# A gated recurrence's bias products on 128 rows, its first block's inputs step by step, and the modulation's products first among the filler

## Chip, cores and metric

One core of a Trainium2 chip. The metric is the device time of one execution in microseconds; lower is better. The kernel before took 1380.88 us, the median of three runs.

## The reference

The whole computation is a quantised feed-forward layer behind a gated recurrence, and behind that a transformer block in hyperbolic geometry with adaptive modulation. What the change touches is the recurrence over 64 steps for a batch of 128, and the modulation vector:

```python
def _L0_cond_ref(h_t, z, W, b, alpha):
    Wh, Wz = W[:, :D], W[:, D:]
    leak = 1.0 - alpha
    def step(h, z_t):
        gate = jax.nn.sigmoid(h @ Wh.T + z_t @ Wz.T + b)
        h_new = jnp.tanh(h * leak + gate * z_t)
        return (h_new, h_new)
    _, hs = jax.lax.scan(step, h_t, jnp.swapaxes(z, 0, 1))
    return jnp.swapaxes(hs, 0, 1)

def _L0_ffn_ref(x, clip_x, ...):
    scale = sigmoid(clip_x) * jnp.max(jnp.abs(x)) / 127.0
...
ada = t_emb @ w_ada + b_ada
sh_msa, sc_msa, g_msa, sh_mlp, sc_mlp, g_mlp = jnp.split(ada, 6, axis=-1)
```

D is 256. t_emb is the conditioning vector, which is also the recurrence's first state. The maximum in the feed-forward layer runs over the whole output of the recurrence, so nothing of that layer can be quantised before step 63 is done.

## The kernel before

**Stages.** The kernel runs the recurrence first (the scan, some 200 us), then the first feed-forward layer up to its global maximum, then a long fused pipeline. Only the scan's code is touched. All DMAs are issued from one queue, SP's, in order.

**The scan.** The state is kept transposed: 256 features lie on 128 partitions in two halves (index c), the batch of 128 along the free dimension. Steps are handled in blocks of four (TS = 4, index n for the block, i for the step in it, t = 4n + i). For each block there are two PSUM tiles pg, one for each half, 128 x 512: four steps of 128 columns.

- z_parts(n) (L406 to L417) puts the input's share into both tiles of a block: for each half one bias product (L413: gate3, the bias split into three bf16 parts on 3 rows, times a tile of ones) and two f32 products of 512 columns (L415). It is a generator that yields after each f32 product. For block 0 it runs to its end before the loop (L419) and leaves the bias product out; later blocks are advanced by one yield in each step of the block before (L451), the rest at the block's end (L461).
- A step adds the state's share: four f32 products of 128 columns (L434; a profile shows each f32 product as two records, so x8). In block 0 two bias products of 128 columns follow (L438).
- Then for each half: sigmoid on ACT (L442), times the input on DVE (L444), plus leak times the old state on DVE (L445), tanh on ACT (L446). L434 of the next step needs the result. L447 keeps a running maximum for the step.

gate3's three rows come by three small DMAs (L206) once DVE has split the bias.

**Filler work.** Everything else that has to be prepared is issued between the steps by a planner in the loop (L452 to L460). There are two generators, products() and pieces(); each yields its pieces with a cost for DVE, ACT and PE. Each step adds a fixed room for each generator (products: 0.3, 0.3, 0.55), and pieces are taken until the room of one engine is used up. products() starts at step 3. The engines run in program order, so a piece lies just behind the step that issued it.

products() holds three things, in this order before the change: the product of two feed-forward weights with each other and with a second weight (L346, wide f32 products of 256 columns, with weights from w_f1T and w_f2), the same weights with a bias (L360, an output of one row; L362 copies it on ACT); the split of that row into three on GpSimd (L364 with L192 and L194, then three DMAs at L365) with a small sum of squares (bsq, L368 to L371); and the modulation (L375 to L391): for each half w of ada, a load of w_ada and of the bias b_ada into the tile ba, six f32 products (L383), three DVE additions into ba (L386, L388), and one DMA that writes ba eight times over to DRAM, 3 MB (L390).

w_f1T, w_f2 and the two halves of w_ada share two buffers (stage2, L233). ba has one buffer, so the second half's load waits until the first half's write has read it.

pieces() quantises and transposes the other weights (L240 to L245 and L92).

**After the scan.** L469 to L473 form the global maximum and its inverse, isx. L488 quantises the states. Its tiles take over the memory of the scan's set-up tiles, which are given back there.

Of the kernel before, what the change touches and what calls it, by code (L numbers as in the profile page):

```python
# [11 lines left out]
F32 = mybir.dt.float32  # L12
F32R = mybir.dt.float32r
BF16 = mybir.dt.bfloat16
# [3 lines left out]
ALU = mybir.AluOpType  # L18
# [4 lines left out]
P = 128  # L23
B, T, D = 128, 64, 256
# [19 lines left out]
AR = 8  # L44
TS = 4
# [25 lines left out]
def tile_kernel(ctx, tc, a, out):  # L71
    nc = tc.nc
    V, S, G_, PE = nc.vector, nc.scalar, nc.gpsimd, nc.tensor
# [68 lines left out]
    with ExitStack() as l0:  # L142
# [15 lines left out]
        with ExitStack() as sc_:  # L158
# [36 lines left out]
                    out.append(part)  # L195
                return out

            gate3 = setup.tile([3, D], BF16, name="gate3")
            ones4 = setup.tile([3, TS * B], BF16, name="ones4")
            V.memset(ones4, 1.0)  # L200

            def to_rows3(parts, dst):
# [22 lines left out]
            def bank():  # L225
                return ps_t.tile([P, 512], F32, name="pt", tag="pt")
# [6 lines left out]
            def stage2(shape, src):  # L233
                t = setup.tile(shape, F32, name="st2", tag="stage2", bufs=2)
                dma(out=t, in_=src)
                return t
# [95 lines left out]
            def products():  # L332

                b1T = setup.tile([P, 8], F32, name="b1T")
                dma(out=b1T, in_=a["b_f1T"])
                s1 = stage2([P, 8, D], a["w_f1T"].rearrange("(c p) k -> p c k", p=P))
                s2 = stage2([P, 8, D], a["w_f2"].rearrange("(c p) k -> p c k", p=P))  # L340
                r2 = setup.tile([1, 2 * D], F32, name="r2")
                for w, s_ in ((0, s1), (1, s2)):
                    pt = bank()
                    for c in range(2):
                        for k in range(8):
                            PE.matmul(pt[:, c * D : (c + 1) * D], lhsT=s1[:, k, c * P : (c + 1) * P],  # L346
                                      rhs=s_[:, k, :], start=(k == 0), stop=(k == 7))
                            yield 0, 0, 0.43
                    gst = setup.tile([P, 2, D], F32, name="gst", tag="gst", bufs=2)
                    S.copy(gst.rearrange("p c k -> p (c k)"), pt)  # L350
                    if w == 0:
                        S.activation(gst[:, 0, P:], pt[:, P:D], AF.Copy, scale=2.0)
                    yield 0, 0.52 + 0.3 * (1 - w), 0
                    for c in range(2):
                        sl = slice(w * D, (w + 1) * D)
                        split((wm[:, 0, c, sl], wm[:, 1, c, sl]), gst[:, c, :])
                        yield 0, 0.35, 0
                    pt = bank()
                    for k in range(8):
                        PE.matmul(pt[:1, :D], lhsT=b1T[:, k : k + 1], rhs=s_[:, k, :], start=(k == 0), stop=(k == 7))  # L360
                        yield 0, 0, 0.43
                    S.activation(r2[:, w * D : (w + 1) * D], pt[:1, :D], AF.Copy, scale=2.0 - w)  # L362
                    yield 0, 0.3, 0
                for i, part in enumerate(split3(r2, 1, G_)):  # L364
                    dma(out=rows3[64 + i : 65 + i, :], in_=part)  # L365
                bsq = setup.tile([P, 8], F32, name="bsq")
                bs1 = setup.tile([P, 1], F32, name="bs1")
                S.activation(bsq, b1T, AF.Square, accum_out=bs1)  # L368
                pt = bank()
                PE.matmul(pt[:, :1], lhsT=ones, rhs=bs1, start=True, stop=True)  # L370
                V.tensor_copy(bb2, pt[:, :1])  # L371
                yield 0.15, 0.3, 0.1


                for w in range(2):  # L375
                    st = stage2([P, 2, 3 * D], a["w_ada"].rearrange("(c p) k -> p c k", p=P)[:, :, w * 3 * D : (w + 1) * 3 * D])
                    ba = setup.tile([P, 3 * D], F32, name="ba", tag="ba", bufs=1)
                    dma(out=ba, in_=a["b_ada"][w * 3 * D : (w + 1) * 3 * D].partition_broadcast(P))
                    for q in range(3):
                        sl = slice(q * D, (q + 1) * D)  # L380
                        pt = bank()
                        for k in range(2):
                            PE.matmul(pt[:, :D], lhsT=h0T[:, k, :], rhs=st[:, k, sl], start=(k == 0), stop=(k == 1))  # L383
                            yield 0, 0, 0.43
                        if q == 1:
                            V.scalar_tensor_tensor(ba[:, sl], pt[:, :D], 1.0, ba[:, sl], ALU.add, ALU.add)  # L386
                        else:
                            V.tensor_tensor(ba[:, sl], pt[:, :D], ba[:, sl], ALU.add)  # L388
                        yield 0.35, 0, 0
                    dma(out=ada_d[:, :, w * 3 * D : (w + 1) * 3 * D],  # L390
                        in_=ba.unsqueeze(1).broadcast_to((P, AR, 3 * D)))  # L391


            vas = []
            for i in range(4):
                va = ep.tile([P, H, 2, HV], F32, name=f"va{i}", tag=f"va{i}", bufs=1)
# [6 lines left out]
            todo, left = [products(), pieces()], [[0.0] * 3] * 2  # L403
            pgs = {}

            def z_parts(n):  # L406

                pgs[n] = [ps_z.tile([P, TS * B], F32, name=f"pg{c}", tag=f"pg{c}") for c in range(2)]
                for c in range(2):
                    sl = slice(c * P, (c + 1) * P)  # L410

                    if n:
                        PE.matmul(pgs[n][c], lhsT=gate3[:, sl], rhs=ones4, start=True, stop=False)  # L413
                    for k in range(2):
                        PE.matmul(pgs[n][c], lhsT=WT[:, 2 + k, sl], rhs=xts[n][:, k, :],  # L415
                                  start=(n == 0 and k == 0), stop=(k == 1))
                        yield  # L417

            for _ in z_parts(0):  # L419
                pass  # L420
            for n in range(T // TS):
                if n + 2 < T // TS:
                    load_x(n + 2)
                xt = xts[n]
                pg = pgs.pop(n)
                ahead = z_parts(n + 1) if n + 1 < T // TS else iter(())
                for i in range(TS):
                    t = n * TS + i
                    st = slice(i * B, (i + 1) * B)
                    z = xt[:, :, st]  # L430
                    hp = h0T if t == 0 else hsT[:, :, t - 1, :]
                    for k in range(2):
                        for c in range(2):
                            lp = PE.matmul(pg[c][:, st], lhsT=WT[:, k, c * P : (c + 1) * P], rhs=hp[:, k, :],  # L434
                                           start=False, stop=False, skip_group_check=True)
                    if n == 0:
                        for c in range(2):
                            lp = PE.matmul(pg[c][:, st], lhsT=gate3[:, c * P : (c + 1) * P], rhs=ones4[:, :B],  # L438
                                           start=False, stop=False, skip_group_check=True)
                    for c in range(2):  # L440
                        gate = wk.tile([P, B], F32, name="gate", tag=f"gate{c}", bufs=2)
                        S.activation(gate, pg[c][:, st], AF.Sigmoid)  # L442
                        with tc.issue_after(lv.ins) if c else nullcontext():
                            V.tensor_tensor(gate, gate, z[:, c, :], ALU.mult)  # L444
                        lv = V.scalar_tensor_tensor(gate, hp[:, c, :], leak[:, c : c + 1], gate, ALU.mult, ALU.add)  # L445
                        ls = S.activation(hsT[:, c, t, :], gate, AF.Tanh)  # L446
                    V.tensor_reduce(hmax[:, t : t + 1], hsT[:, :, t, :], AX.XY, ALU.max,  # L447
                                    apply_absolute_value=True)

                    with tc.issue_after(lv.ins), tc.issue_after(ls.ins), tc.issue_after(lp.ins):  # L450
                        next(ahead, None)  # L451
                        for q in range(2):  # L452
                            if t < CFG["hold"][q]:
                                continue
                            left[q] = [min(l, 0.0) + r for l, r in zip(left[q], CFG["room"][q])]
                            while min(left[q]) > 0:
                                cost = next(todo[q], None)
                                if cost is None:
                                    break
                                left[q] = [l - c for l, c in zip(left[q], cost)]  # L460
                for _ in ahead:  # L461
                    pass
# [765 lines left out]
```

## Time and profile before

| what | us |
|---|---|
| median of three runs | 1380.88 |
| lowest and highest | 1379.86, 1386.22 |
| profiled execution, its own time | 1374.36 |
| its span, first to last instruction | 1372.6 |
| first sigmoid (step 0) | 14.28 |
| first sigmoid of step 4 | 25.87 |
| first sigmoid of step 61 | 186.29 |
| last running maximum of the scan (L447) ends | 195.22 |
| first L488 | 201.66 |

Times inside an execution are counted from the span's start. A line of the chain of waits gives start, length and the work on the chain; a line of the timeline gives start, length, engine, line, operation, tiles, shapes and count. Records of one line that follow each other are merged there, with the count behind the x. PE stands for matmuls on TensorE, PEld for its weight loads, SPq for the DMA queue's issues, ACT for the scalar engine, DVE for the vector engine and POOL for GpSimd.

### The profile page before, as it was taken

What the parts mean: (1) busy time and instruction counts of PE and PEld (TensorE: products, weight loads), DVE (VectorE), ACT (ScalarE), POOL (GpSimd) and SP (SyncE); (2) the same over time, 40 slices, a digit from 0 to 9 for tenths busy, and PEclk for the clock granted to TensorE, in tenths of its full rate; (3) what the DMA queues carried; (4) which work ended last, traced back from release to release, by engine and by line L of the source; (5) the groups of instructions that cost most, each with busy time, mean ns of one, the idle gap of its engine ahead of it and who ended that gap; (6) DMA issues with size and microseconds to landing.
All of it is one profiled execution on the core that took longest, in us unless ns stands there. A gap on an engine that the chain in (4) does not pass through costs nothing.

```text
span 1372.6 us, 23851 instructions
## 1 busy us (share of the span) xinstructions
PE 1096.8 (80%) x7380; PEld 744.0 (54%) x7380; DVE 1145.4 (83%) x3544; ACT 827.0 (60%) x2428; POOL 844.6 (62%) x1043
## 2 busy tenths in 40 slices
PE   7999957984589789878879798888887888964654
PEld 4656542332366566655657576666655656643442
DVE  5666669997778787888998999999899989899573
ACT  2545438982377568666768666776675777752331
POOL 3111207865688766687868878686686785765441
PEclk9999989995599789889999798997998989986765
DMA  7112245669733441233344334322414231323211
GB/s 236 54 54 85 70 196 195 257 265 283 225 96 120 124 145 49 90 116 117 98 130 125 116 113 146 108 92 90 126 63 124 70 104 51 97 74 96 72 47 46
DMA packets 119306, 163.66 MB, mean 119 GB/s; under 512 B 10885, under 2 KB 72074, under 8 KB 119178
## 3 DMA queue, kind: packets, MB, share of 16 engines
q1 hardware_dynamic: 119178, 162.13, 37.0%
q8 instruction: 58, 0.95, 0.3%
q14 instruction: 70, 0.57, 0.1%
HBM read 115.94 MB, written 46.14 MB: 118 GB/s over the span
## 4 chain that ended last, share of the span: by engine, by line
DVE 44%; PE 21%; POOL 14%; DMA 8%; issue 6%; ACT 6%; SPq 1%; POOLq 0%; DVEq 0%; ACTq 0%
DMA ada<-ada_d 5%; PE pg L434 4%; DVE u L797 4%; PE pg L415 3%; DVE u L724 2%; DVE u L725 2%; DVE junk L743 2%; DVE nh L920 2%; DVE u L618 2%; DVE bn L703 2%; DVE u L1052 2%; POOL r L640 2%; PE pgate L527 1%; PE qk L915 1%; POOL u L737 1%
## 5 line engine op out<-in xcount | busy, mean ns | idle before, releaser
L609 ACT ACTIVATE junk<-u 128x256 bf16<-128x256 f32 x432 | 183.8, 428 | 162.1 <-DVE u L725 49.4
L915 PE MATMUL qk<-wqkv,uT 128*128 128x512 f32 (+1 forms) x768 | 194.8, 391 | 12.3 <-DVE uT L906 6.4
L737 POOL TENSOR_TENSOR u<-u,ada 128x256 f32<-128x256 f32 x128 | 105.7, 827 | 80.9 <-ACT junk L609 73.4
L915 PEld LDWEIGHTS qk<-wqkv,uT 128*128 128x128 f32 x768 | 132.9, 209 | 40.2 <-DVE uT L906 12.1
L966 PE MATMUL sc<-qM,kT 64*64 64x256 f32 x1024 | 128.1, 419 | 20.9 <-ACT kT L956 11.6
L1040 PE MATMUL ml<-wm,uT 128*128 128x512 f32 (+1 forms) x384 | 120.9, 454 | 0.0
L983 PE MATMUL ao<-va,e 128*64 128x34 f32 x2048 | 90.1, 241 | 32.9 <-DVE u L1014 17.8
L983 PEld LDWEIGHTS ao<-va,e 128*64 128x64 f32 x2048 | 79.5, 155 | 59.6 <-DVE u L1014 19.4
L1040 PEld LDWEIGHTS ml<-wm,uT 128*128 128x128 f32 x384 | 83.7, 221 | 47.3 <-issue 25.3
L616 ACT ACTIVATE qM<-sc,mhead 128x256 f32<-128x256 f32 x256 | 102.0, 495 | 11.5 <-PE sc L92 11.3
L880 PE MATMUL dn<-wdT,hq 128*128 128x256 bf16 (+1 forms) x384 | 66.3, 314 | 45.9 <-DVE x L882 20.4
L513 POOL TENSOR_TENSOR hv<-uv,sil 128x512 f32<-128x512 f32 x44 | 57.6, 1312 | 66.2 <-DVE am L516 48.5
L945 POOL TENSOR_TENSOR va<-qkv,comb 64x256 f32<-64x256 f32 x128 | 88.3, 690 | 9.9 <-PE ao L983 4.2
L966 PEld LDWEIGHTS sc<-qM,kT 64*64 64x64 f32 x1024 | 56.5, 143 | 63.1 <-ACT kT L956 17.7
L609 ACT ACTIVATION_READ_ACCUMULATOR junk<-u 128x1 f32 x432 | 87.9, 203 | 0.0
L974 ACT ACTIVATE e<-sc 128x512 f32<-128x512 f32 x128 | 74.7, 606 | 19.4 <-PE ao L983 9.7
L434 PE MATMUL pg<-hsT,WT 128*128 128x128 f32 x504 | 75.3, 289 | 9.4 <-ACT hsT L446 9.0
L434 PEld LDWEIGHTS pg<-hsT,WT 128*128 128x128 f32 x504 | 64.7, 191 | 31.4 <-ACT hsT L446 28.6
L1094 PE MATMUL fp<-wfT,yT 128*128 128x256 f32 x256 | 78.7, 439 | 0.0
L941 POOL TENSOR_TENSOR qkv<-qkv,comb 128x512 f32<-128x512 f32 x64 | 70.2, 1110 | 12.3 <-DVE comb L932 3.0
L620 POOL TENSOR_SCALAR hb<-hl,cu 128x1280 int8<-128x1280 f32 x64 | 64.2, 1008 | 21.4 <-DMA hl<-h_d 14.0
L880 PEld LDWEIGHTS <-hq 128*128 128x128 bf16 (+1 forms) x384 | 37.2, 108 | 73.1 <-issue 37.5
(286 smaller groups left out, 3192.6 us busy)
## 6 DMA issues: line engine op xcount, KB each, us to landing
ada<-ada_d SPq DMA_DIRECT2D x128, 256.0 KB, 3.5
h_d<-hv SPq DMA_DIRECT2D x80, 256.0 KB, 2.1
hl<-h_d SPq DMA_DIRECT2D x32, 640.0 KB, 4.3
ada<-ada_d SPq DMA_DIRECT2D x128, 128.0 KB, 2.4
xt<-in_xT_dram SPq DMA_DIRECT2D x16, 512.0 KB, 4.5
xr<-in_x_dram SPq DMA_DIRECT2D x32, 256.0 KB, 4.3
x_d<-x SPq DMA_DIRECT2D x32, 256.0 KB, 3.1
xt<-x_d SPq DMA_DIRECT2D x32, 256.0 KB, 2.8
```

The source lines that it names most:

```text
L434: lp = PE.matmul(pg[c][:, st], lhsT=WT[:, k, c * P : (c + 1) * P], rhs=hp[:, k, :], start=False, stop=False, skip_group_check=True)
L609: S.activation(junk, src, AF.Square, accum_out=acc)
L616: S.activation(dst, src, AF.Copy, scale=by)
L737: ENG[pick(f"gate{which}", g)].tensor_tensor(av, av, gb, ALU.mult)
L880: PE.matmul(py[:, i * D : (i + 1) * D], lhsT=hq[r, j, i * P : (i + 1) * P], rhs=wdT[r, j, :], start=(i == 0 and j == 0), stop=(j == 5), sk ...
L915: PE.matmul(pm[:, :n_], lhsT=uT[:, z, k, cs], rhs=wqkv[:, w, k, lo:hi], start=False, stop=(k == 1 and q == 2))
L945: ENG[pick("va", g)].tensor_tensor(va[r, :, s, 0:HD], qkv[r, xy, 512:768].rearrange("p (h d) -> p h d", d=HD), bc_in(comb[r, xy * 48 + 32 ...
L966: PE.matmul(sc[rr][s * T : (s + 1) * T, c * 256 : (c + 1) * 256].rearrange("p (v t) -> p v t", v=4), lhsT=kTs[xy][r, c, s * T : (s + 1) * ...
L974: S.activation(e.rearrange("p c v t -> p (c v t)"), sc[rr], AF.Exp, scale=1.0 / math.sqrt(HD))
L983: PE.matmul(pv[xy * T : (xy + 1) * T, hh], lhsT=E[2 * xy + hh // 4][:, c, hh % 4, :], rhs=vas[(2 * h2 + xy) % 4][:, c * 8 + hh], start=Tru ...
L1040: PE.matmul(pm[:, cs], lhsT=uT[:, z, k, i * P : (i + 1) * P], rhs=wm[:, w, k, cs], start=False, stop=(k == 1 and q == 2))
L1094: PE.matmul(o, lhsT=yT[:, 2 * i + c, :], rhs=wfT[:, c, :], start=False, stop=(c == 1))
```

## The change

It has three parts.

1. gate3 and ones4 become tiles of 128 rows. gate3 is filled with zeros first, and its three rows are written as before; the bias products multiply 128 rows, of which 125 add zero.
2. Block 0's inputs are multiplied step by step. z_first(i) issues four f32 products of 128 columns: step 0's before the loop, the next step's within each step. z_parts is used from block 1 on alone, and in block 0 it is advanced from step 1 on, not from step 0 on.
3. The modulation's loop moves to the front of products(), unchanged but for ba, which gets two buffers.

```diff
-            gate3 = setup.tile([3, D], BF16, name="gate3")
-            ones4 = setup.tile([3, TS * B], BF16, name="ones4")
+            gate3 = setup.tile([P, D], BF16, name="gate3")
+            V.memset(gate3, 0.0)
+            ones4 = setup.tile([P, TS * B], BF16, name="ones4")
...
             def products():
+                for w in range(2):
+                    st = stage2([P, 2, 3 * D], a["w_ada"]...)
+                    ba = setup.tile([P, 3 * D], F32, name="ba", tag="ba", bufs=2)
...
+                    dma(out=ada_d[:, :, w * 3 * D : (w + 1) * 3 * D],
+                        in_=ba.unsqueeze(1).broadcast_to((P, AR, 3 * D)))
...
-                for w in range(2):
-                    st = stage2([P, 2, 3 * D], a["w_ada"]...)
-                    ba = setup.tile([P, 3 * D], F32, name="ba", tag="ba", bufs=1)
...
+            def z_first(i):
+                st = slice(i * B, (i + 1) * B)
+                for c in range(2):
+                    for k in range(2):
+                        PE.matmul(pgs[0][c][:, st], lhsT=WT[:, 2 + k, c * P : (c + 1) * P], rhs=xts[0][:, k, st],
+                                  start=(i == 0 and k == 0), stop=False, skip_group_check=True)
+
             def z_parts(n):
...
-                    if n:
-                        PE.matmul(pgs[n][c], lhsT=gate3[:, sl], rhs=ones4, start=True, stop=False)
+                    PE.matmul(pgs[n][c], lhsT=gate3[:, sl], rhs=ones4, start=True, stop=False)
                     for k in range(2):
                         PE.matmul(pgs[n][c], lhsT=WT[:, 2 + k, sl], rhs=xts[n][:, k, :],
-                                  start=(n == 0 and k == 0), stop=(k == 1))
+                                  start=False, stop=(k == 1))
                         yield
 
-            for _ in z_parts(0):
-                pass
+            pgs[0] = [ps_z.tile([P, TS * B], F32, name=f"pg{c}", tag=f"pg{c}") for c in range(2)]
+            z_first(0)
             for n in range(T // TS):
...
-                pg = pgs.pop(n)
+                pg = pgs[n]
...
-                        next(ahead, None)
+                        if n == 0 and i + 1 < TS:
+                            z_first(i + 1)
+                        if n or i:
+                            next(ahead, None)
```

More of the change, by code (lines that the diff above doesn't have):

```diff
@@ L332, in products @@
             def products():
+                for w in range(2):
+                    st = stage2([P, 2, 3 * D], a["w_ada"].rearrange("(c p) k -> p c k", p=P)[:, :, w * 3 * D : (w + 1) * 3 * D])
+                    ba = setup.tile([P, 3 * D], F32, name="ba", tag="ba", bufs=2)
+                    dma(out=ba, in_=a["b_ada"][w * 3 * D : (w + 1) * 3 * D].partition_broadcast(P))
+                    for q in range(3):
+                        sl = slice(q * D, (q + 1) * D)
+                        pt = bank()
+                        for k in range(2):
+                            PE.matmul(pt[:, :D], lhsT=h0T[:, k, :], rhs=st[:, k, sl], start=(k == 0), stop=(k == 1))
+                            yield 0, 0, 0.43
+                        if q == 1:
+                            V.scalar_tensor_tensor(ba[:, sl], pt[:, :D], 1.0, ba[:, sl], ALU.add, ALU.add)
+                        else:
+                            V.tensor_tensor(ba[:, sl], pt[:, :D], ba[:, sl], ALU.add)
+                        yield 0.35, 0, 0
+                    dma(out=ada_d[:, :, w * 3 * D : (w + 1) * 3 * D],
+                        in_=ba.unsqueeze(1).broadcast_to((P, AR, 3 * D)))
                 b1T = setup.tile([P, 8], F32, name="b1T")
@@ L372, in products @@
                 yield 0.15, 0.3, 0.1
-                for w in range(2):
-                    st = stage2([P, 2, 3 * D], a["w_ada"].rearrange("(c p) k -> p c k", p=P)[:, :, w * 3 * D : (w + 1) * 3 * D])
-                    ba = setup.tile([P, 3 * D], F32, name="ba", tag="ba", bufs=1)
[L378 to L391, printed above, removed]
             vas = []
@@ L404, in tile_kernel @@
             pgs = {}
+            def z_first(i):
+                st = slice(i * B, (i + 1) * B)
+                for c in range(2):
+                    for k in range(2):
+                        PE.matmul(pgs[0][c][:, st], lhsT=WT[:, 2 + k, c * P : (c + 1) * P], rhs=xts[0][:, k, st],
+                                  start=(i == 0 and k == 0), stop=False, skip_group_check=True)
             def z_parts(n):
```

## The prediction

> **What bounds the kernel now.** I read the page for the span, then the windows over the recurrent scan, then the chain of waits there, then the timeline at both its ends. Only the first 202 us can change: the global maximum at the end of the scan (L469 to L473) gates the quantisation at L488, so time won or lost before it moves everything behind it, whose instructions stay the same.
>
> Page, then windows (the stretch, its length, busy time of PE, PEld, DVE, ACT, POOL, granted clock, DMA share, GB/s):
>
> ```profile
> span 1372.6 us, 23851 instructions
> ...
> ada_d<-ba SPq DMA_DIRECT2D x2, 3072.0 KB, 9.3
> ```
>
> ```profile
> 14.28:25.87 11.59, 10.86 (x53) 6.57 (x51) 8.62 (x32) 4.37 (x18) 2.77 (x6) 1.00 0.99 320
> 25.87:183.79 157.92, 153.36 (x750) 96.70 (x748) 104.12 (x320) 77.48 (x263) 27.95 (x45) 1.00 0.26 82
> 183.79:201.66 17.87, 6.29 (x33) 4.45 (x31) 8.77 (x30) 4.70 (x16) 0.00 (x0) 0.75 0.54 210
> ```
>
> Steps 0 to 3, steps 4 to 59, and the tail. PE is full in the middle and idle two thirds of the tail. The chain in step 8 (start, length):
>
> ```profile
> 37.64 0.32 PE pg L413
> 37.96 1.06 PE pg L415 x2
> 39.01 0.43 PE pt L346 x2
> 39.44 0.22 PE pt L92 x2
> 39.66 0.89 PE pg L434 x8
> 40.56 0.86 PE pg L415 x2
> ```
>
> The first five lines add to 2.92 us, which is exactly the distance of step 8's first sigmoid (37.45) from step 9's (40.37). The input product costs 0.86 without a bias product in front and 0.32 + 1.06 = 1.38 with one: **a 3-row bias product costs 0.52**. Steps with little filler take 2.50 (sigmoid, multiply, add, tanh, then L434). So a step is the larger of 2.50 and its PE sum: 0.89 (L434) + 0.86 (L415) + 0.52 (bias, even steps) + 0.43 per wide product (L346 or L383, 256 columns) + 0.22 per transposed pair; two L360 cost 0.52, four 0.95, and the switch back 0.15 to 0.20. This hits every step that DVE doesn't stretch to 0.01 us. Over steps 4 to 60 it gives 155.4; the sigmoids say 160.4, and the other 5.0 is DVE work slowed beside POOL.
>
> The chain at the tail, then three places of the timeline and a row of tile pg (min/median/max ns):
>
> ```profile
> 175.50 9.31 DMA ada_d<-ba
> 184.82 3.42 DMA ba<-in_b_ada_dram
> 188.36 0.42 DVE ba L388
> ...
> 192.24 5.52 DMA ada_d<-ba
> 197.76 3.80 issue
> 201.66 1.76 DVE q L488 x3
> ```
>
> ```profile
> 9.14 0.53 SPq L206 DMA_DIRECT2D gate<-s3p  x1
> ```
>
> ```profile
> 14.02 0.28 PE L438 MATMUL pg<-ones,gate 3*128 3x128 bf16 x2
> ```
>
> ```profile
> 669.04 0.27 PE L1092 MATMUL fp<-rows,ones 128*128 128x256 bf16 x1
> 669.15 1.03 PE L1094 MATMUL fp<-wfT,yT 128*128 128x256 f32 x4
> ```
>
> ```profile
> L415 PE MATMUL pg<-xt,WT x128: 592/595/1190, 7.4 to 181.6; 128*128 128x512 f32 x128
> ```
>
> The second bias tile waits for the first one's write; step 61 then takes 4.00 instead of 2.50. The second write starts at 192.24 and, at 9.3, lands at 201.55: just when L488 starts, though its scale was ready at 197.76.
>
> **128-row bias products.** L1092 is such a product with 256 columns; L1094 follows 0.11 later, its bare streaming time. For 512 columns that makes 0.22 and no charge on the neighbours: 0.31 less, in 28 even steps from 4 to 58. Bounds: 0 (row count doesn't matter) to 0.31. I take 0.31, since L1092 is the same operation. The added memset of gate3 and the taller ones4 lie before 2.8 us, where DVE waits for cb until 6.8: nothing; without that cover, some 0.3 each (the 128x256 memset of L118 took 0.27).
>
> The Trainium skill, page "TensorE: Matmul & The Clock Gate", section "Why this matters for your kernels", says the opposite: a single K=32 product takes the time of a K=128 one. By it the bias term is 0 and the sum below 4.8 smaller, at −3.9. The trace disagrees where products follow each other: 0.52 against the 0.22 from L1092's spacing.
>
> **The order of products().** The planner adds 0.55 of PE room a step and takes pieces until it is used, so the order follows by arithmetic. The modulation's 12 products and 6 DVE additions move from steps 51–62 to 3–14, L346 and L360 from 3–48 to 15–60, L362 to 61, split3 and bsq from 50 to 62. With the new order and 0.21 for a bias product, these steps exceed 2.50: 0.11 in 5, 11, 13, 15, 20, 39, 50; 0.14 in 33, 37; 0.18 in 56; 0.32 or 0.33 in 7, 9, 18, 25, 42, 46, 49; 0.35 in 34, 36; 0.40 in 35, 55; 0.54 in 22; 0.61 in 58; 0.78 in 32. That is 6.9 over 57 × 2.50 = 142.5, so 149.4: **−6.0**, of which 4.8 is the bias term (the new order with 0.52 gives 154.3; 28 × 0.31 would be 8.7, but what falls below 2.50 earns nothing). In steps 4 and 14 an addition (0.42) meets a quantised row (0.41 + 0.15 + 0.15) and hmax (0.41) in the 1.2 that L444 and L445 leave free of 2.50: **+0.6**. The other DVE delays stay, split3's 0.9 + 0.4 (steps 50 and 51) now in 62 and 63.
>
> DMAs: two w_ada loads and two ba loads go first on SP; w_f1T and w_f2 wait for their two buffers, free after steps 7 and 13, and are needed at 15 and 39 (5.6 us each): hidden. While SP waits for the first of these buffers, near 37, the x load that was issued at 36.21 and bias rows of L206 may stand behind it; x is needed at 48.7, the rows after the scan. The two 9.3 us writes start near 40 and 57. That x load comes ahead of the first. The one of 58.28 is needed at 70.85: behind the write it lands near 57 + 9.3 + 3.7 = 70. Hidden by under 1 us.
>
> **The tail.** Step 61 loses its wait: **−1.5**. L488 loses 201.66 − 197.76: **−3.9**. What is late next: split3 runs 4.6 us on POOL after L362 (156.56 to 161.13), and its last row, with 0.5 of issue and 4.4 to land, could arrive 0.6 after L488 is ready; whether L488's tile lies on it no view tells: 0 to 0.6, I take **+0.3**. With less filler in steps 60 to 63 PE's clock may halve earlier than before (granted 1.00 in 185 to 192, 0.53 in 192 to 202), doubling L434 once or twice, 0.7 each: 0 to 1.4, **+0.5**.
>
> **The first block.** z_first(0) is a quarter of eight products that took 5.79; they start at 7.40, at half rate (1190 against 595 ns). PE then reaches L438 near 10.8. But gate3's third row is issued at 9.14 and lands 4.4 later, at 13.55, and L438 ran at 14.02: only **−0.4** is to be had. Inside the block the inputs return: step 0 keeps its latency, 2.88 less some 0.2 for the two cheaper L438, 2.7; from one sigmoid to the next PE does in step 1 z_first 0.86, bias and input product 0.21 + 0.86, L434 0.89, L438 0.15, together 2.97; in step 2 the same without the bias, 2.76, and 2.9 with its DVE delay; in step 3 0.21 + 0.86, two wide products 0.86, the block's last input product 0.86 and L434 0.89, 3.7. That is 12.3 against 11.6: **+0.7**. PE now idles from 10.8 to 13.6, so the next steps may run at half clock: 0 (full rate granted at once) to 2 (L434 and filler doubled over some 3 us of PE's work), **+1.0**.
>
> **Sum:** −6.0 + 0.6 − 1.5 − 3.9 + 0.3 + 0.5 − 0.4 + 0.7 + 1.0 = **−8.7**. The profiled execution took 1374.36 (span 1372.6), so 1365.7. It is 6.5 below the median of the runs; from that median I forecast **1372.2**.
>
> **Rivals.**
> *The writes get in the way of x (slower side).* If SP places a write and the next 1 MB load (5.6) ahead of an x load, x lands 9.3 + 5.6 + 3.7 = 18.6 after its turn, against 12.6 of slack: 6.0 late, and PE stands in L415 with the whole scan behind it. Twice: +12, 1384.2, and with 2 for a cold PE after each gap 1388.2. It decides once x is late by 8.7 in all. For: one queue, in order. Against: 54 to 85 GB/s in slices 2 to 5 of the page, and buffers that come free before the writes start.
> *The tail only swaps its wait.* split3 runs a step (2.5) later than planned and L488 waits 3.1 for its rows: +2.8, 1375.0. For: POOL slows DVE and itself there. Against: SP has no x load to serve by then.
> *The row count is not what costs.* If a 3-row product streams like a 128-row one and the 0.20 extra on L415 comes from changing between bf16 and f32, the bias term is gone: +4.8, 1377.0. Against: L1092 to L1094 changes type and costs nothing. This is where the page named above would lead.
> *A cold start.* PE stays at half clock through steps 1 and 2: sums 2.97 and 2.76 double, +5.7 in place of +1.0: 1376.9. For: L415 ran its first four microseconds at half rate. Against: L434 and z_first doubled fill the steps, as L415 did before the clock rose.
> The Trainium skill's page "TensorE: Matmul & The Clock Gate", same section, asks for about 4 us of unbroken work to release the clock and no gap above 3 us; here 3.4 us of work and a gap of 2.8 stand before step 0, which leans to this rival.
>
> **Chances.** Forecast 0.60 (own range 1368.5 to 1375.5), x late 0.07, swapped wait 0.13, row count 0.10, cold start 0.10. A run of this kernel can't tell less than about 0.5%, 6.9 us, from no change. Below 1374.0 lies 0.85 of the forecast's case, half of the swapped wait, a third of the cold start and a little of the others: 0.63 faster. Above 1387.8: x late with a cold PE, 0.05. Same: 0.32. The range reaches from the full gain with no cold steps (−8.7 without the terms +1.0, +0.5, +0.3 and +0.6 is −11.1, and 4 more for the rest of the kernel, whose three runs lie 6.4 apart) to the row count's and the cold start's 1377.0 with 2.5 of that spread: 1365 to 1379.5.
>
> **What would show it.** The 3*128 shapes gone; L415 at 0.86 in every step; even steps without filler still 2.50; both ada_d writes before 70 us; step 61 at 2.5; L488 within 3 us of the scale; step 0 at 13.9. I am wrong if an x load or w_f1T ends an idle time of PE, if the steps from 4 to 60 last over 157, or if the time behind L488 changes.

## The result and the profile after

The changed kernel takes 1366.91 us, the median of six runs (1361.47 to 1370.59), against 1380.74 for the kernel before (1378.60 to 1386.22). The ratio is 0.9894 with a 95% interval of 0.9869 to 0.9918: 13.8 us faster. Its profiled execution took 1362.89 us.

In the changed kernel's code the step's products L434 are L442, the bias products L413 and L438 are L421 and L446, L415 is L423 (blocks 1 on) and L413 (z_first), the sigmoid is L450, L444 to L447 are L452 to L455, L383 is L344 and L488 is L499.

The page of the changed kernel, its span:

```profile
span 1361.0 us, 23892 instructions
```

It is 11.6 below before's 1372.6. Windows of the changed kernel for steps 0 to 3, steps 4 to 60, and from step 61 to L499 (the stretch, its length, busy time of PE, PEld, DVE, ACT, POOL, granted clock, DMA share, GB/s):

```profile
13.94:27.43 13.49, 13.18 (x77) 10.99 (x77) 8.38 (x32) 4.34 (x17) 3.03 (x7) 0.87 0.94 317
27.43:180.96 153.53, 148.50 (x760) 99.10 (x758) 105.32 (x327) 77.87 (x264) 23.40 (x40) 1.00 0.31 107
180.96:192.29 11.33, 4.74 (x23) 3.83 (x21) 7.23 (x24) 3.98 (x15) 4.27 (x5) 0.68 0.00 0
```

The first stretch is longer than before's 11.59 and no longer at full clock; the tail from step 61 is 4.0 shorter than before's 15.4 (186.29 to 201.66) and moves next to nothing by DMA (share 0.00). The chain of waits of the changed kernel, in its start, in steps 8 and 9, and in its tail (start, length, what):

```profile
9.60 3.94 DMA gate<-s3p
13.55 0.14 issue
13.68 0.23 PE pg L446
13.91 0.02 issue
13.94 0.29 ACT gate L450
14.22 0.04 issue
14.27 1.99 PE pg L413 x8
16.25 1.69 PE pg L442 x8
17.95 0.11 PE pg L446 x2
18.06 0.22 PE pg L421
18.27 0.86 PE pg L423 x2
19.13 0.89 PE pg L413 x8
...
39.38 0.21 PE pg L421
39.59 0.86 PE pg L423 x2
40.45 0.22 PE pt L92 x2
40.67 1.20 PE pg L442 x8
41.88 0.86 PE pg L423 x2
...
184.10 1.13 DVE gate L453
...
185.62 1.66 PE pg L442 x6
...
189.33 0.43 DVE hmax L455
...
192.08 0.21 DVE sux L486
192.29 1.12 DVE q L499 x2
```

The reader sees four things. The first sigmoid still waits for gate3's third row, and the two groups of products behind it take 1.99 and 1.69 where the same z_first takes 0.89 a step later: half clock. In step 8 the bias product costs 0.21 and the input product behind it 0.86, where before it was 0.32 and 1.06. Step 62 is stretched by L453 and by a half-clock L442. And L499 follows the last of the scale's instructions (L486) directly; no DMA stands in the tail's chain.

Here are the stretches of all profiled executions. "0-3" runs from step 0's first sigmoid to step 4's, "61-63" from step 61's first sigmoid to the start of the last running maximum, "to q" from there to the first quantisation (before's L488), whose start is "q"; "behind" is from q to the span's end. In the changed kernel q is 192.20; the chain counts L499 from 192.29, where L486 ends. Each row is one execution. All in us.

| kernel | first sigmoid | 0-3 | 4-60 | 61-63 | to q | q | behind | span |
|---|---|---|---|---|---|---|---|---|
| before | 14.28 | 11.59 | 160.43 | 8.51 | 6.86 | 201.66 | 1170.92 | 1372.58 |
| after | 13.94 | 13.50 | 153.53 | 8.37 | 2.87 | 192.20 | 1168.78 | 1360.98 |
| e1_rows | 14.64 | 11.00 | 156.19 | 9.15 | 6.34 | 197.32 | 1178.76 | 1376.08 |
| e2_order | 14.89 | 11.58 | 157.84 | 8.32 | 2.87 | 195.50 | 1179.64 | 1375.14 |
| e3_zfirst | 13.98 | 16.36 | 160.09 | 9.46 | 6.37 | 206.26 | 1196.89 | 1403.16 |
| e4_rows_order | 14.35 | 11.00 | 152.99 | 8.37 | 2.87 | 189.57 | 1173.21 | 1362.78 |
| f1_before_recip | 15.40 | 11.56 | 160.24 | 8.19 | 6.91 | 202.31 | 1184.26 | 1386.57 |
| f2_before_recip4 | 15.63 | 11.56 | 160.66 | 9.41 | 6.34 | 203.61 | 1176.89 | 1380.50 |
| f3_rows_order_recip | 14.27 | 11.00 | 153.45 | 8.36 | 2.87 | 189.94 | 1181.63 | 1371.57 |
| f4_rows_order_recip4 | 14.70 | 10.99 | 153.42 | 8.37 | 2.87 | 190.34 | 1175.52 | 1365.86 |
| g1_after_again | 14.46 | 13.19 | 153.57 | 8.37 | 2.87 | 192.45 | 1168.65 | 1361.10 |
| g2_rows_order_again | 14.58 | 11.00 | 153.57 | 8.32 | 2.87 | 190.34 | 1171.08 | 1361.43 |
| g3_rows_zfirst | 14.17 | 13.45 | 155.70 | 9.17 | 6.50 | 198.99 | 1186.94 | 1385.94 |
| g4_warm | 14.20 | 12.19 | 153.65 | 9.50 | 2.87 | 192.40 | 1174.76 | 1367.16 |

So the scan gave 9.5 us (201.66 to 192.20), and the median fell by 13.8. The rest lies behind q, in code that the change does not touch.

### The profile page after: what moved, and what is told of

The parts are those of the page before. It is cut to its first block, busy times and chain, and to the rows that moved or that the text cites. A ratio compares the mean times of both kernels' runs of the same rounds, so it can differ in the third digit from the quotient of the medians.

```text
span 1361.0 us, 23892 instructions
## 1 busy us (share of the span) xinstructions
PE 1103.2 (81%) x7404; PEld 758.7 (56%) x7404; DVE 1138.0 (84%) x3545; ACT 827.7 (61%) x2428; POOL 841.5 (62%) x1043
## 4 chain that ended last, share of the span: by engine, by line
DVE 46%; PE 25%; POOL 12%; DMA 6%; issue 5%; ACT 5%; SPq 1%; DVEq 0%; POOLq 0%; ACTq 0%
PE pg L442 5%; DMA ada<-ada_d 3%; DVE u L808 3%; PE pg L423 3%; DVE am L527 2%; DVE u L735 2%; PE qk L926 2%; DVE u L629 2%; PE ml L1051 2%; DVE nh L931 2%; PE sc L977 2%; DVE bn L714 2%; DVE u L736 2%; DVE junk L754 2%; DVE hv L526 2%
## 5 line engine op out<-in xcount | busy, mean ns | idle before, releaser
L926 PE MATMUL qk<-wqkv,uT 128*128 128x512 f32 (+1 forms) x768 | 189.1, 386 | 8.0 <-DVE uT L917 4.1
L977 PE MATMUL sc<-qM,kT 64*64 64x256 f32 x1024 | 140.4, 452 | 21.7 <-ACT kT L967 19.7
L748 POOL TENSOR_TENSOR u<-u,ada 128x256 f32<-128x256 f32 x128 | 100.3, 786 | 65.2 <-ACT junk L620 60.3
L1051 PE MATMUL ml<-wm,uT 128*128 128x512 f32 (+1 forms) x384 | 117.8, 447 | 0.0
L994 PE MATMUL ao<-va,e 128*64 128x34 f32 x2048 | 94.9, 247 | 27.2 <-DVE u L1025 14.7
L994 PEld LDWEIGHTS ao<-va,e 128*64 128x64 f32 x2048 | 83.7, 162 | 55.9 <-DVE u L1025 17.3
L891 PE MATMUL dn<-wdT,hq 128*128 128x256 bf16 (+1 forms) x384 | 69.8, 329 | 42.6 <-DVE x L893 17.6
L977 PEld LDWEIGHTS sc<-qM,kT 64*64 64x64 f32 x1024 | 61.1, 153 | 68.7 <-ACT kT L967 28.3
L442 PE MATMUL pg<-hsT,WT 128*128 128x128 f32 x504 | 76.5, 293 | 8.2 <-ACT hsT L454 7.7
L442 PEld LDWEIGHTS pg<-hsT,WT 128*128 128x128 f32 x504 | 66.2, 195 | 26.6 <-ACT hsT L454 23.4
L631 POOL TENSOR_SCALAR hb<-hl,cu 128x1280 int8<-128x1280 f32 x64 | 65.0, 1022 | 21.9 <-DMA hl<-h_d 15.4
L928 ACT COPY qkv<-qk 128x512 f32<-128x512 f32 (+1 forms) x128 | 61.2, 502 | 27.5 <-PE qk L926 27.0
```

The source lines that it names most:

```text
L748: ENG[pick(f"gate{which}", g)].tensor_tensor(av, av, gb, ALU.mult)
L891: PE.matmul(py[:, i * D : (i + 1) * D], lhsT=hq[r, j, i * P : (i + 1) * P], rhs=wdT[r, j, :], start=(i == 0 and j == 0), stop=(j == 5), sk ...
L926: PE.matmul(pm[:, :n_], lhsT=uT[:, z, k, cs], rhs=wqkv[:, w, k, lo:hi], start=False, stop=(k == 1 and q == 2))
L977: PE.matmul(sc[rr][s * T : (s + 1) * T, c * 256 : (c + 1) * 256].rearrange("p (v t) -> p v t", v=4), lhsT=kTs[xy][r, c, s * T : (s + 1) * ...
L994: PE.matmul(pv[xy * T : (xy + 1) * T, hh], lhsT=E[2 * xy + hh // 4][:, c, hh % 4, :], rhs=vas[(2 * h2 + xy) % 4][:, c * 8 + hh], start=Tru ...
L1051: PE.matmul(pm[:, cs], lhsT=uT[:, z, k, i * P : (i + 1) * P], rhs=wm[:, w, k, cs], start=False, stop=(k == 1 and q == 2))
```

## The experiments

The first four take the change apart; the next four leave the scan alone and disturb only what lies behind it; the last four repeat, complete the set and test the clock.

**e1_rows: the 128-row bias products alone.**

```diff
-            gate3 = setup.tile([3, D], BF16, name="gate3")
-            ones4 = setup.tile([3, TS * B], BF16, name="ones4")
+            gate3 = setup.tile([P, D], BF16, name="gate3")
+            V.memset(gate3, 0.0)
+            ones4 = setup.tile([P, TS * B], BF16, name="ones4")
```

> Before with the 128-row bias tiles alone; the instructions keep the order of before. My theory (a 3-row product costs 0.52 us, a 128-row one 0.22, and a step is the larger of 2.50 and its PE sum): steps 4 to 60 take 5 us less (160.4 to about 155.3), L488 starts near 196 instead of 201.7. Rival (the row count is not what costs): steps 4 to 60 within 0.5 of 160.4 and L488 at 201.5. What lies behind L488 took 1170.9 in the profiled execution of before: if only the order of the instructions decides there, it stays within 3 of that.

Measured: 1378.13 us against 1382.62, ratio 0.9976 (0.9952 to 0.9999); steps 4 to 60 fell by 4.2 and q by 4.3. The chain of waits of this kernel in step 8, whose counterpart of before is shown in the prediction:

```profile
37.45 0.22 PE pg L414
37.66 0.86 PE pg L416 x2
38.52 0.43 PE pt L347 x2
38.95 0.22 PE pt L92 x2
39.17 0.89 PE pg L435 x8
```

The same filler stands behind the products, so the two steps compare directly: 2.62 instead of 2.92. The row count is what cost 0.30. This kernel's instructions stand in before's order on every engine, also behind the scan, with one memset more. Even so its profiled time behind q is 1178.76, 7.8 above before's and not within the 3 that was expected: single executions of one order scatter that much, so times behind q are compared by medians below.

**e2_order: the modulation first, with two bias tiles, alone.** The loop over w with its loads, products and writes as in the change's diff; the bias products stay at 3 rows.

```diff
             def products():
+                for w in range(2):
...
+                    ba = setup.tile([P, 3 * D], F32, name="ba", tag="ba", bufs=2)
...
-                for w in range(2):
...
-                    ba = setup.tile([P, 3 * D], F32, name="ba", tag="ba", bufs=1)
```

> Before with the modulation's products in front and two ba tiles alone. My theory: step 61 near 2.5 instead of 4.00, L488 2.4 us behind the last running maximum instead of 6.4, steps 4 to 60 within 1 of 160.4, L488 near 196. Rival (the tail swaps its wait for the split of the bias row): L488 3 or more behind the scale. Behind L488: 1170.9 if the order of the rest had stayed; it did not, so up to 5 either way. A rival for the part behind the scan: the early write of the modulation makes it faster, here and in the kernel with both parts, by 2 to 4, and in no other.

Measured: 1373.77, ratio 0.9934 (0.9914 to 0.9954). q came 6.2 earlier: 2.6 in steps 4 to 60, where less than 1 was expected, and from 6.86 to 2.87 behind the start of the last maximum. Both waits for the modulation are gone.

**e3_zfirst: the first block step by step, alone.**

```diff
+            def z_first(i):
...
-            for _ in z_parts(0):
-                pass
+            z_first(0)
...
-                        next(ahead, None)
+                        if n == 0 and i + 1 < TS:
+                            z_first(i + 1)
+                        if n or i:
+                            next(ahead, None)
```

> Before with block 0's inputs step by step alone. My theory: the first sigmoid moves from 14.28 to about 13.9 only, since gate3's last row lands at 13.55, PE's clock halves in the gap, and steps 0 to 3 take 1.9 us or more longer; L488 near 203.5. Rival (the shorter start pays): first sigmoid near 11 or steps 0 to 3 as before, L488 at 200 or below.

Measured: 1402.07, ratio 1.0147 (1.0118 to 1.0176), far slower than any theory had it. Only 4.6 of the 19.5 us lie in the scan. The timeline of this kernel's PE (start, length, engine, line, operation, tiles, shapes, count):

```profile
7.30 2.05 PE L412 MATMUL pg<-xt,WT 128*128 128x128 f32 x8 [7.30 <-DMA xt<-in_xT_dram]
9.14 1.91 PE L441 MATMUL pg<-h0T,WT 128*128 128x128 f32 x8
13.69 0.37 PE L445 MATMUL pg<-ones,gate 3*128 3x128 bf16 x2 [2.64 <-DMA gate<-s3p]
14.31 2.08 PE L412 MATMUL pg<-xt,WT 128*128 128x128 f32 x8 [0.26 <-ACT gate L449]
16.18 1.92 PE L441 MATMUL pg<-hsT,WT 128*128 128x128 f32 x8
...
20.64 1.84 PE L412 MATMUL pg<-xt,WT 128*128 128x128 f32 x8
22.32 1.06 PE L441 MATMUL pg<-hsT,WT 128*128 128x128 f32 x8
```

Here the products run at half rate until 22.3, through steps 0 and 1 and beyond: steps 0 to 3 take 16.36, 4.8 more than before. They ran at half rate ahead of the idle time of 2.64 too (2.05 and 1.91 for eight records, against 1.06 at full rate): this execution did not lose the full clock in the gap, as its theory had it, but did not have it before 22.3. This is the prediction's cold start, in another kernel than the one predicted.

**e4_rows_order: both without z_first** (the edits of e1 and e2 together).

> The changed kernel without its step-by-step inputs (128-row tiles and the new order of the products). My theory: block 0 as before (step 4 at 25.6 to 25.9 instead of 27.43), steps 4 to 60 as in the changed kernel (153.6), L488 near 190.7 instead of 192.3. Behind L488 it has the order of instructions of the kernel with the new order alone, and should take the same time as that one within 3. Rival (the parts don't add): L488 at 192 or later.

Measured: 1365.47, ratio 0.9877 (0.9849 to 0.9905). From e2 to e4, which differ in the bias rows alone, steps 4 to 60 fall by 4.85. q comes at 189.57, 2.6 earlier than in the changed kernel: in the scan, z_first loses. The time behind q was expected within 3 of e2's; the two profiled executions lie 6.4 apart, the medians less q 2.4.

**The order behind the scan.** Before these four runs the sums already failed to close: e1 won 4.3 us before q and 4.5 in its median, but e3 lost 4.6 before q and 19.5 in its median. The instruction order of the programs gave the reason. In e2, e3, e4 and the changed kernel the scheduler issues the untouched code behind the scan in another order, from inside the first feed-forward layer on, on every engine. Two theories remained: the order itself changes the time, or the modulation's earlier write helps the later stages. To tell them apart, the scan was left as it was and a reciprocal of one column (some 0.2 us) was repeated behind it, which the scheduler has to place:

```diff
         V.reciprocal(cu, sh[:, 0:1])
+        V.reciprocal(cu, sh[:, 0:1])
         V.tensor_scalar(sdh, sd_bc, sh[:, 0:1], None, ALU.mult)
```

f1 and f2 are the kernel before with it twice and four times in all; f3 and f4 are e4 with the same.

> Before, with the reciprocal that makes cu (behind the feed-forward layer's global maximum, some 0.2 us) issued twice. The scan's instructions and their order stay; every engine's order behind that point is another one. Theory (the order that the scheduler finds for the fused part decides its length): L488 at 201.7 and 197.7 to 201.9 as before, but the median differs from before's by 3 or more, in either direction. Rival (the early modulation makes the fused part faster): the median within 2 of before's.

> Before, with that reciprocal issued four times: a third order of the fused part, the scan as before. Theory: a median that differs by 3 or more from before's or from the kernel with two reciprocals. Rival: within 2 of both (0.5 for the three extra reciprocals).

> 128-row tiles and the new order of the products, with the reciprocal issued twice: the scan of the kernel without the step-by-step inputs (L488 near 189.6), another order behind it. Theory: the time behind L488, which by the medians was about 5 shorter there than in before, changes by 3 or more. Rival (early modulation): it stays 3 to 5 shorter than before's.

> As the kernel before this one, with the reciprocal issued four times. Theory: yet another time behind L488; over the kernels with the early modulation and those without, these times overlap. Rival: all kernels with the early modulation lie 3 to 5 below all those without.

Measured: f1 1387.39 against 1382.09, ratio 1.0046 (1.0026 to 1.0066); f2 1373.98, 0.9932 (0.9902 to 0.9962); f3 1373.18, 0.9927 (0.9897 to 0.9957); f4 1370.96, 0.9916 (0.9885 to 0.9947), the last two beside e4's 0.9877. One repeated reciprocal makes the kernel before 5.3 us slower, three make it 8.1 faster. The timeline of POOL in the kernel before, and then in f2, at the same place of the work:

```profile
378.89 1.66 POOL L640 TENSOR_TENSOR lnaln<-tln,nhalf 128x8 f32<-128x8 f32 x1 [3.71 <-DVE tln L695]
380.66 1.63 POOL L720 TENSOR_SCALAR u<-x,nm,lnaln 128x256 f32<-128x256 f32 x3
382.25 1.07 POOL L941 TENSOR_TENSOR qkv<-qkv,comb 128x512 f32<-128x512 f32 x1
```

```profile
381.60 1.67 POOL L643 TENSOR_TENSOR lnaln<-tln,nhalf 128x8 f32<-128x8 f32 x1 [2.96 <-DVE tln L698]
383.23 1.07 POOL L944 TENSOR_TENSOR qkv<-qkv,comb 128x512 f32<-128x512 f32 x1
384.24 1.31 POOL L948 TENSOR_TENSOR va<-qkv,comb 64x256 f32<-64x256 f32 x2
```

Behind lnaln the one kernel does three u first and then qkv, the other qkv at once. One such swap proves nothing on its own; that the median moves by 5 and 8 us when such swaps and the reciprocals themselves (0.2 each) are all that changes does. The median less the profiled q gives the time behind q:

| order behind q | kernels | median less q |
|---|---|---|
| before's | before, e1 | 1180.4, 1180.8 |
| e2's | e2, e4, g2, g4 | 1178.3, 1175.9, 1173.8, 1174.8 |
| the changed kernel's | after, g1 | 1174.7, 1171.7 |
| e3's | e3, g3 | 1195.8, 1198.4 |
| others, before's scan | f1, f2 | 1185.1, 1170.4 |
| others, e4's scan | f3, f4 | 1183.2, 1180.6 |

(The row of before uses its median beside f1 and f2, 1382.09; beside the changed kernel's six runs it is 1179.1.) Kernels with one order lie within 4.5 us of each other; the orders lie up to 28 apart. The early write does not decide it: f2 writes late and has the shortest time of all, f3 writes early and has one of the longer ones.

**g1, g2: the changed kernel and e4 again, on one chip; g3: e1 and e3 together.**

> The changed kernel again, on the same chip as the next ones. Theory: 0.985 to 0.992 of before, as in the result; first sigmoid near 13.9, steps 0 to 3 at 13 or more, L488 within 1.5 of 192.2.

> 128-row tiles and the new order of the products, without the step-by-step inputs, again. Theory: L488 about 2.5 earlier than in the changed kernel, and a median of about 1366, no slower than the changed kernel's on this chip. Rival (its lead in the first block is noise of one execution): L488 at 191.5 or later.

> 128-row tiles and the step-by-step inputs, with the products in their old order. Behind the scan it has the same instructions in the same order as the kernel with the step-by-step inputs alone (1402.1). Theory: slower than before by some 15 us although its scan is 2 to 4 shorter, since that order of the fused part costs about 15. Rival (the 15 came from something else in that run): within 5 of before.

Measured against 1382.90: g1 1364.16, ratio 0.9871 (0.9832 to 0.9909); g2 1364.17, 0.9873 (0.9842 to 0.9904); g3 1397.34, 1.0111 (1.0073 to 1.0148). The changed kernel and the one without z_first tie: what z_first loses in the scan (2.1 at q) its order behind the scan gives back. g3 has e3's order exactly and is as slow behind q as e3, with q at 198.99, 7 us earlier than e3's.

**g4_warm: the changed kernel with PE kept busy before step 0.** Two products of 512 columns, whose result nothing reads, go behind z_first(0). They cut PE's idle time before step 0's bias products from 2.51 to 0.92.

```diff
             z_first(0)
+            pt = bank()
+            for k in range(2):
+                PE.matmul(pt, lhsT=WT[:, k, :P], rhs=xts[0][:, k, :], start=(k == 0), stop=(k == 1))
```

> The changed kernel with two more f32 products of 512 columns behind z_first(0), whose result nothing reads: PE has work until gate3's last row lands. Theory (part of the first block's loss is the clock that halves in that gap): the clock stays full from about 11 on, steps 0 to 3 take 12.4 instead of 13.5, L488 near 191. Rival (the loss is the products moved into the block alone): steps 0 to 3 stay at 13.5.

Measured: 1367.19, ratio 0.9890 (0.9852 to 0.9929). The windows of this kernel for steps 0 to 3 and for 4 to 60:

```profile
14.20:26.39 12.19, 11.88 (x77) 9.56 (x77) 8.42 (x32) 4.35 (x17) 2.81 (x6) 1.00 0.99 333
26.39:180.04 153.65, 148.49 (x760) 99.09 (x758) 105.44 (x327) 77.88 (x265) 23.75 (x40) 1.00 0.32 107
```

With most of the gap filled the clock stays full, and steps 0 to 3 take 12.19 instead of 13.50. So the cold clock cost the changed kernel 1.3. The rest is 0.6 over before's 11.59; over the 11.00 of the kernels with 128-row tiles and without z_first (e1, e4) it is 1.2, the price of the inputs that came back into the block. The whole kernel did not gain: q came at 192.40 and not near 191, since steps 61 to 63 took 9.50 instead of 8.37, with the clock half from 181.8 on instead of 185.1, and the code behind q has e2's order.

## Why the prediction was right, and where it failed

The direction and the range held (1366.91 in 1365 to 1379.5); the forecast of 1372.2 was 5.3 too high, and 0.8 of that lies in the scan. The narrower range of the forecast's own case (1368.5 to 1375.5) was missed by 1.6.

| term | forecast | measured |
|---|---|---|
| first sigmoid | -0.4 | -0.34 |
| steps 0 to 3, products moved | +0.7 | +0.6 (g4) |
| steps 0 to 3, cold clock | +1.0 | +1.3 (g4) |
| steps 4 to 60 | -6.0 + 0.6, less the 1.3 of split3 that leaves them: -6.7 | -6.9 |
| steps 61 to 63 | -1.5 + 0.5 and the 1.3 of split3: +0.3 | -0.1 |
| last maximum to q | -3.9 + 0.3 | -4.0 |
| sum, to q | -8.7 | -9.5 |
| behind q | 0 | -2.1 profiled, -4.4 by medians |

**Bias products.** Right in mechanism and nearly in size: 0.52 to 0.21, 4.85 us between e2 and e4 against the 4.9 that the sums with 0.52 and with 0.21 gave (154.3 and 149.4). The 4.85 is flattered by steps 4 and 5, which took 5.72 in e4 but 6.15 to 6.26 in the other executions of its scan (f3, f4, g2); steps 6 to 60 fell by 4.3 to 4.4 in all four. L1092's spacing, far from the scan, was the right row to price it by. In the old order (e1) steps 6 to 60 fell by 4.6, and steps 4 and 5 gave 0.3 back. Not every even step gains: 42 and 50 stay as they were, and in step 47 a DVE delay comes out that PE's longer work had kept smaller (the product with the input meets an instruction on POOL and takes 0.94 instead of 0.63).

**Order of products().** Right. The order alone gave 2.6 (e2), where the step sums with DVE's share make 1.8; the other 0.8 was not traced. Steps 4 to 60 took 4.1 more than PE's 149.4; assumed for DVE were 5.6 less 1.3.

**First block.** Right in sign and nearly in size: with all three parts the first sigmoid wins 0.3 and steps 0 to 3 lose 1.9. z_first's own loss is larger: beside e4 it wins 0.4 and loses 2.5, of which the 128-row tiles hide 0.6. The step that limited it is the one named, the landing of gate3's third row. The cold start is a price with a spread: 1.3 in the changed kernel and, as an estimate, 3.6 in e3 (its 4.8 less the 1.2 for the inputs), with nearly the same work and idle time of PE before it (2.51 and 2.64). Windows of the changed kernel show where its clock was granted:

```profile
10.98:14.39 3.41, 0.59 (x5) 0.25 (x4) 0.14 (x1) 0.45 (x2) 0.00 (x0) 1.00 0.79 207
14.39:17.80 3.41, 3.41 (x17) 3.35 (x18) 1.93 (x8) 0.71 (x3) 0.89 (x2) 0.50 0.98 303
17.80:27.43 9.63, 9.63 (x61) 7.52 (x60) 6.31 (x24) 3.19 (x12) 2.14 (x5) 1.00 0.93 321
```

PE worked for 0.59 of the first 3.41 us, and the next 3.41 came at half clock. g1 and g3 show the same pattern, with steps 0 to 3 at 13.19 and 13.45; e3 alone got its full clock only at 22.3. Why it came so late there was not tried.

**Tail.** Step 61 went from 4.00 to 2.50 and L499 directly follows the scale. Step 62 went from 2.55 to 3.84, which was priced as split3's share and a half-clock L434; both came. The timeline of the changed kernel, POOL's work at that place and SP's DMAs around the two writes:

```profile
183.89 1.18 POOL L194 TENSOR_TENSOR r<-r,s3p 1x512 f32<-1x512 f32 x1
...
41.13 0.62 SPq L351 DMA_DIRECT2D ada_d<-ba  x1
48.24 0.37 SPq L181 DMA_DIRECT2D xt<-in_xT_dram  x1
...
56.78 0.56 SPq L351 DMA_DIRECT2D ada_d<-ba  x1
58.67 0.37 SPq L181 DMA_DIRECT2D xt<-in_xT_dram  x1
```

L453 of step 62, 0.35 elsewhere, starts at 184.10 during L194 on POOL and ends at 185.23, 0.16 behind L194's end. The third row of split3 was cast by 187.8 and L499 did not wait for it.

**Rivals.** The writes started at 41.13 and 56.78, as forecast, and no x load ended an idle time of PE: x late fell. The swapped wait fell with L499's start right behind the scale. The row count fell in e1: between 128-row products, 3 rows cost 0.30 more. The Trainium skill's page "TensorE: Matmul & The Clock Gate", section "Why this matters for your kernels", says that a single product with K=32 takes the time of one with K=128; no run here has such a product alone, and for products that follow each other e1's 0.30 disagrees. The cold start came in part.

**The step that failed** is the first paragraph's: "Only the first 202 us can change", because what follows are instructions "that stay the same". The instructions are the same, their order is not: the scheduler orders the whole program, and an edit in the scan gave the code behind it another order. In the changed kernel this was worth 4.4 us by the medians beside the first six runs and 9.5 by those beside g1 (1382.90 less 201.66, against 1364.16 less 192.45); in e3's order it cost 15 to 17. With that order the same scan would have ended near 1388 (an estimate: 192.2 plus e3's 1195.8), outside the range; that the range held is partly luck. The forecast's test, that it would be wrong if the time behind L488 changes, caught it. The median fell by more than the sum mostly for this reason; the scan gave only 0.8 more.

**What stays open.** Which of the reordered instructions make e3's order 15 us slower is not known. Matched instruction by instruction, from q on, g3 stays within 5 us of before (medians over stretches of 60 us) up to 700 us behind q and lies 18 to 28 behind it from 1020 on, so most of the loss comes late. The stretch from q to the first use of the feed-forward layer's second scale (sdh) took 107.3 to 108.5 us in all kernels with the modulation first and 106.2 to 106.9 in the others; its cause was not tried.

## What to carry to other kernels

Price a small product by what it does to its neighbours: the sum of a step's PE work against the step's latency gave this change, up to a fixed point in the profile, to within a microsecond. But where a scheduler orders the program, an edit also reshuffles all that comes later, and this lottery was here as large as the gain (from 10 us less to 17 more of some 1380); to judge an edit, measure it up to a fixed point in the profile, and compare program orders before reading the total. A shorter start is worth nothing while its last input lands at the same time, and the idle time that it opens can cost the clock.

## What the runs showed of the hardware

- A bf16 product of 3 rows and 512 columns between f32 products of 128 rows took 0.32 and added 0.20 to the pair behind it; padded with zero rows to 128 it took 0.21 to 0.22 and added nothing.
- After an idle time of 2.51 us on PE the changed kernel's granted clock was half for 3.41 us (14.39 to 17.80), although it had been full in the 3.41 us ahead of that. e3, with 2.64 us idle, ran its products at half rate before the gap and after it, until 22.3. Two products of 512 columns, which left 0.92 us idle, kept the clock full (g4).
- A two-input DVE instruction that starts during a two-input POOL instruction ended only after it, by 0.14 to 0.16: L453 of step 62 took 1.13 instead of 0.35 in the changed kernel, and the product with the input in step 47 took 0.63 in before and 0.94 in e1, with 0.28 to 0.29 elsewhere. The Trainium skill's page "SBUF — State Buffer", section "Terms", says of the port pair that these engines share that the loser blocks fully and does not share bandwidth; these three places agree.
